# Layer 0 of a four-layer image kernel: sampled values through DRAM, two vertical taps in one matmul, and two small edits in layer 2

## The chip, the core and the metric

The kernel runs on one core of a Trainium2 chip. The metric is device time in microseconds (us), the median of several runs of the whole program. Five engines work side by side and meet only at semaphores: TensorE (PE, with its weight loads PEld), VectorE (DVE), ScalarE (ACT), GpSimd (POOL) and SyncE (SP, which here only issues DMA transfers). POOL issues DMA transfers as well.

## What is computed

Four residual layers run one after another on an image batch. Only layer 0 and layer 2 matter here. Layer 0 is a group norm, two 1x1 convolutions, and two deformable 3x3 convolutions of 180 channels in 10 groups of 18, on 2 images of 96x96:

```python
xr = conv1x1(x, w_reduce, b_reduce)
offs = conv1x1(xr, w_offset, b_offset)
off_w, off_h = (offs[:, :cm], offs[:, cm:])
f_w = deform_conv2d(xr, off_w, w_dcnw, b_dcnw)
f_h = deform_conv2d(xr, off_h, w_dcnh, b_dcnh)
...
val = gather(y0, x0, (1 - dy) * (1 - dx)) + gather(y0, x0 + 1, (1 - dy) * dx) + ...
patches = val.reshape(Bx, C, KK, Hx, Wx)
out = jnp.einsum('bikhw,oik->bohw', patches, weight.reshape(Cout, Cin, KK))
```

So each of the two convolutions (called cv = 0 and 1 in the kernel) samples every channel at 9 displaced places (taps) for each pixel, by bilinear weights, and then multiplies 180 channels x 9 taps by a weight matrix. Layer 2 is a bidirectional recurrence over 9216 positions (a running maximum and two running sums), a gate, a layer norm over channels and a 1x1 convolution.

## The kernel before

**Tiles of layer 0.** `near0` does one image. It walks 79 tiles of up to 128 positions: four of a narrow right edge (kind 2), 72 of 8 rows x 16 columns (kind 0; three make a chunk, two chunks a strip of 8 rows), three of the bottom edge (kind 1). Image 0 runs with the preparation of image 1 (`reduce0`, "aside") woven in; image 1 runs alone.

**Stages.** Each tile has three stages l = 0, 1, 2: groups 0-3, 4-7, 8-9. For a stage, POOL subtracts step positions from offsets (`hats`, L541), ACT turns that into hat weights (L548, L550), DVE multiplies vertical by horizontal weights (`products`, L571), PE transposes them into PSUM banks `pt` (`turn`, L587), ACT and DVE copy them out (L595, L593). `sample` then multiplies them on PE by 8x8 image windows `xw` (L634) for 8 patches of 4x4 pixels, and ACT copies the result from `pt` to `val` (L655): 8 copies of 288 columns in stages 0 and 1, 4 of 288 in stage 2, where two patches share a bank (`together`). There are five banks `pt`, which `turn` and `sample` share.

**Gathering.** A sampled group of 18 channels lies in its own 32 lanes. `gathered` moves it, SBUF to SBUF, on SP's queue (L672, L679): groups 0-6 into `main`, 126 lanes dense, groups 7-9 into `more`, three groups (54 lanes) at lane 0 for cv 0 and at lane 64 for cv 1. That is 26 transfers a tile, each of 18 lanes.

**Convolving.** `convolve` (L702) multiplies by the weights and accumulates in PSUM (`pf`), each tap at its own shifted place: 27 (output block, tap) pairs for `main` and 27 for `more`, both for cv 0 and cv 1 side by side, 128 columns each. It is a generator: in tile n+1, PE does the first half of tile n's `main` matmuls after stage 0's sampling, the second half after stage 1's, all of `more` after stage 2's. So per tile PE's order is: 36 transposes, sample 0, main, 36 transposes, sample 1, main, 18 transposes, sample 2, more.

**Orders.** In `near0` the order of PE, ACT and DVE is that of the program; POOL and SP are ordered by the scheduler. After each strip `done` and `finish` add borders, reduce, and let POOL add the bias and store the strip (L718 to L782). Windows for a later tile are 16 small DMA issues on POOL (`windows`, L559).

**Layer 2.** 18 chunks of 512 positions, each in three channel groups (54 iterations), forward and then backward. All four engines are in program order. `load` fetches the chunk's input `xt` (two buffers per image) six iterations ahead; in the backward half the gate reads the same `xt` (L1690 follows its matmul), so a buffer stays in use until its chunk's last gate. `weighted` (L1736) makes four exponentials on ACT (L1731, L1733): b, a, eb, ea. In the backward half a and ea share a ring of two PSUM banks, so the a of the next iteration waits until the scans of this one (L1755) have read theirs. Later on ACT in the same iteration come a logarithm and an exponential (`logged`, L1800, L1801), and DVE's `scaled` (L1813) waits for them.

Of the kernel before, what the change touches and what calls it, by code (L numbers as in the profile page):

```python
# [6 lines left out]
F32 = mybir.dt.float32  # L7
# [11 lines left out]
P = 128  # L19
CH = 96  # L20
CM, MH = 180, 90
# [13 lines left out]
LT = P  # L35
# [5 lines left out]
MAIN = 7  # L41
CO = 64
# [19 lines left out]
class Net:  # L62
# [283 lines left out]
    def near_constants(self, wn, at_d):  # L346
# [101 lines left out]
        wl = wn.tile([P, KK, NO * CO], F32, name="wl")  # L448
        nc.gpsimd.memset(wl, 0.0)
        nc.gpsimd.memset(wd[:, :, :, CM:], 0.0)  # L450
        for cv in range(2):
            src = ins["w_dcn"][cv].rearrange("(g t c) o -> g c t o", g=G, t=KK)
            for g in range(G):
                at = g * CG if g < MAIN else cv * 64 + (g - MAIN) * CG
                nc.gpsimd.dma_start(
                    out=wd[at : at + CG, cv, :, :CM] if g < MAIN else wl[at : at + CG, :, :CM],
                    in_=src[g],
                )
# [16 lines left out]
    def near0(self, b, xp_d, o_d, u_d, f_d, sums, far, top, con, aside=None):  # L475
# [5 lines left out]
        with ExitStack() as ctx:  # L481
# [4 lines left out]
            sv = ctx.enter_context(tc.tile_pool(name=f"n0v{b}", bufs=3))  # L486
# [111 lines left out]
            def split(kind, size, patches):  # L598

                rows, columns = size  # L600
                n = (len(patches) + 3) // 4
                return n, *((rows // n, columns) if kind != 1 else (rows, columns // n))

            def sample(sts, xw, l, kind, parts, patches):
# [8 lines left out]
                vals = []  # L613
                for e in range(2):
                    val = sv.tile([P, KK * LT], F32, name=f"val{e}")
                    vals.append(
                        val[:, : 2 * KK * rows * columns].rearrange(
                            "p (s r c) -> p s r c", r=rows, c=columns
                        )
                    )  # L620
                together = 1 if l < 2 else min(2, len(patches))
                for i in range(min(4, len(patches))):
# [24 lines left out]
                    for e in range(2):  # L647
                        to = vals[e][: nh * 64, :n]
                        if kind == 2:
                            to = to[:, :, vr : vr + together * nr]  # L650
                            to = to.rearrange("p s (j r) c -> p j s (r c)", j=together)
                        else:
                            to = to[:, :, :, vc : vc + together * ncol]
                            to = to.rearrange("p s r (j c) -> p j (s r) c", j=together)
                        nc.scalar.copy(  # L655
                            to,
                            pvs[e][: nh * 64, : together * w].rearrange(
                                "p (j a b) -> p j a b", j=together, b=to.shape[3]
                            ),
                        )  # L660
                return vals

            def gathered(main, more, l, vals, nh):

                for e in range(2):
                    val = vals[e].rearrange("p s r c -> p s (r c)")
                    for q in range(2):
                        g = 4 * l + (2 * q if l < 2 else 0) + e
                        for h in range(nh):
                            from_ = slice(h * 64 + q * 32, h * 64 + q * 32 + CG)  # L670
                            if g < MAIN:
                                nc.sync.dma_start(  # L672
                                    out=main[g * CG : (g + 1) * CG, h], in_=val[from_]
                                )
                                continue
                            for cv in range(2) if l < 2 else (q,):
                                lane = cv * 64 + (g - MAIN) * CG
                                s0 = cv * KK if l < 2 else 0
                                nc.sync.dma_start(  # L679
                                    out=more[lane : lane + CG, h], in_=val[from_, s0 : s0 + KK]  # L680
                                )

            def convolve(pf, main, more, kind, e, parts, first, last):

                nh, rows, columns = parts
                todo = [(m, t) for m in range(NO) for t in range(KK)]
                cut = len(todo) // 2
                for l, part in ((0, todo[:cut]), (0, todo[cut:]), (1, todo)):
                    for m, t in part:
                        ky, kx = 2 - t // 3, 2 - t % 3  # L690
                        y, x = ((ky, 16 * e + kx), (ky, 32 * e + kx), (32 * e + ky, kx))[kind]
                        for cv in range(2):
                            at = slice(cv * 64, cv * 64 + (G - MAIN) * CG) if l else slice(0, MAIN * CG)
                            wt = con["wl"][at, t] if l else con["wd"][:, cv, t]
                            if kind == 1:
                                to = pf[cv * CO : (cv + 1) * CO, m, y : y + rows, x : x + nh * columns]
                                to = to.rearrange("p r (h c) -> p h r c", h=nh)
                            else:
                                to = pf[cv * CO : (cv + 1) * CO, m, y : y + nh * rows, x : x + columns]
                                to = to.rearrange("p (h r) c -> p h r c", h=nh)  # L700
                            took = more[at, :, t] if l else main[:, :, cv * KK + t]
                            nc.tensor.matmul(  # L702
                                to,
                                wt[:, m * CO : (m + 1) * CO],
                                took.rearrange("p h (r c) -> p h r c", c=columns),
                                start=first and l == 0 and t == 0,
                                stop=last and l == 1 and t == KK - 1,
                                skip_group_check=True,
                                tile_position=(at.start, cv * CO),
                            )  # L710
                    yield

# [32 lines left out]
            ed = s1.tile([P, 3, H + 4, 4], F32, name="ed")  # L745
            nt = STRIPS * 6
            def plan(kind, i, j):
# [3 lines left out]
                for e in range(4 if kind == 2 else 3):  # L751
                    patches, corners = [], []
                    for a in range(8 if kind < 2 or e < 3 else 1):
                        r, c = a // (columns // 4) * 4, a % (columns // 4) * 4
                        y = (8 * i, W, 32 * e)[kind] + r
# [97 lines left out]
            for k, (n, l) in enumerate(stages):  # L853
# [15 lines left out]
                if k + 1 < len(stages):  # L869
# [4 lines left out]
                    make(turned + 1)  # L874
                if l == 0:
                    main = sb.tile([MAIN * CG, 2 * KK * LT], F32, name="main")
                    more = sb.tile([P, KK * LT], F32, name="more")
                    parts = split(kind, size, patches)
                    half = parts[1] * parts[2]
                    main, more = (  # L880
                        v[:, : parts[0] * m * half].rearrange("p (h s n) -> p h s n", s=m, n=half)
                        for v, m in ((main, 2 * KK), (more, KK))
                    )
                vals = sample(sts.pop(k), xws[n], l, kind, parts, patches)
                gathered(main, more, l, vals, parts[0])
# [609 lines left out]
    def layer2(self, x, out, stats):  # L1495
# [10 lines left out]
        with ExitStack() as ctx:  # L1506
# [5 lines left out]
            sy = ctx.enter_context(tc.tile_pool(name="l2y", bufs=2))  # L1512
            pk = ctx.enter_context(tc.tile_pool(name="l2k", bufs=2, space=PSUM))
# [141 lines left out]
            def load(i):  # L1655
                back, c, g = seq[i]
                if g == 0:
                    xts[back, c] = []
                    for b in range(B):
                        xt = sb.tile([CH, 2, T], F32, name=f"xt{b}")  # L1660
# [75 lines left out]
            def weighted(i):  # L1736
                if seq[i][0]:
# [756 lines left out]
```

## Time and profile before

The kernel takes 10528.72 us (median of 3 runs, 10526.48 to 10530.25). The profiled execution took 10534.88 us, with a span of 10533.1 us from first to last instruction. Busy time by stretch of the span:

| stretch (us) | what | length | PE | DVE | ACT | POOL | PE clock | DMA share | GB/s |
|---|---|---|---|---|---|---|---|---|---|
| 0-390 | layer 0, preparation | 390 | 190 | 188 | 14 | 59 | 0.84 | 0.74 | 133 |
| 390-3030 | layer 0, image 0 | 2640 | 2515 | 2057 | 1673 | 1781 | 0.98 | 0.38 | 91 |
| 3030-5205 | layer 0, image 1 | 2175 | 2135 | 1599 | 1502 | 1369 | 0.99 | 0.37 | 90 |
| 5205-6115 | end of layer 0, layer 1 | 910 | 617 | 567 | 116 | 179 | 0.81 | 0.39 | 117 |
| 6115-6465 | layer 2, forward | 350 | 243 | 315 | 311 | 266 | 0.92 | 0.49 | 168 |
| 6465-7150 | layer 2, backward | 685 | 536 | 570 | 441 | 513 | 0.85 | 0.39 | 117 |
| 7150-10533 | layer 3 | 3383 | 3130 | 2963 | 1952 | 2845 | 0.85 | 0.71 | 163 |

How to read the profile: "PE L702 MATMUL pf<-more,wl 54*64 54x128" is the instruction at line 702, its output and inputs by the program's names, the weight's shape and the moving operand's (lanes x columns). A float32 matmul shows as two instructions, a transpose as one. Brackets at the end of a timeline line give how long the engine stood still before it and what ended that. The share of DMA is the mean over 16 DMA engines; "issue" lines on SP and POOL show how long an engine took to issue transfers, not how long these took.

### The profile page before, as it was taken

To read this page: it belongs to the slowest core of one execution; us is meant where nothing else is said; L and a number is where in the kernel's file an instruction comes from. 1 tells how busy PE (TensorE), PEld (TensorE's weight loads), DVE (VectorE), ACT (ScalarE), POOL (GpSimd) and SP (SyncE) were. 2 spreads that over 40 slices of the span, in tenths; PEclk is the share of its full clock that TensorE was granted. 3 is DMA by queue.
4 is the path that set the end of the run, shared out by engine and by line. 5 is a ranking of instruction groups with operands and counts; after the bars stand their busy time and mean duration, and the time that the engine had idled before them with its cause. 6 is when DMAs were issued, how large, how long until landed. Compare 5 with 4: busy or idle time off the path is not lost. (4 is left out here: it accounts for less than half of the span.)

```text
span 10533.1 us, 230262 instructions
## 1 busy us (share of the span) xinstructions
PE 9365.6 (89%) x92614; PEld 5530.4 (53%) x92614; DVE 8257.2 (78%) x8704; ACT 6008.3 (57%) x11216; POOL 7013.2 (67%) x5527
## 2 busy tenths in 40 slices
PE   4799999999989999999966776787999999999998
PEld 3588888888868888888822222222222222222222
DVE  4677777777677777777755788883999999999999
ACT  0366666666666676666600168663666666666664
POOL 1466766766555666666511258773888888888888
PEclk8899999999989999999978888886888888888887
DMA  8433434433323333333344344432777777777776
GB/s 146 90 93 95 97 96 95 97 96 95 78 68 89 93 90 91 89 93 90 80 128 127 109 153 150 123 120 72 170 172 170 172 171 172 173 170 171 172 169 148
DMA packets 601281, 1282.72 MB, mean 122 GB/s; under 512 B 238700, under 2 KB 321888, under 8 KB 543808
## 3 DMA queue, kind: packets, MB, share of 16 engines
q1 hardware_dynamic: 387560, 1081.12, 41.7%
q0 software_dynamic: 103808, 133.18, 5.7%
q10 hardware_dynamic: 108840, 53.57, 2.0%
q8 instruction: 739, 12.11, 0.5%
q14 instruction: 334, 2.74, 0.1%
HBM read 786.57 MB, written 231.25 MB: 97 GB/s over the span
## 5 line engine op out<-in xcount | busy, mean ns | idle before, releaser
L571 DVE TENSOR_TENSOR sp<-h 128x2304 f32<-128x2304 f32 x790 | 2162.2, 2769 | 25.7 <-ACT h L550 25.7
L2236 DVE TENSOR_TENSOR_SCAN h<-da,state,bu 128x512 f32<-128x512 f32 x1632 | 1959.5, 1262 | 238.2 <-ACT da L2226 231.9
L595 ACT COPY st<-pt 128x512 f32<-128x512 f32 (+1 forms) x2370 | 1218.7, 517 | 1310.3 <-PE pt L587 1241.3
L2203 POOL TENSOR_TENSOR bu<-bu,bs 128x2048 f32<-128x2048 f32 x432 | 1954.0, 4523 | 16.9 <-DMA bu<-ud 16.8
L593 DVE COPY st<-pt 128x512 f32<-128x512 f32 x1580 | 1062.0, 687 | 985.2 <-PE pt L587 968.3
L587 PE MATMUL pt<-ident,sp 128*128 128x128 f32 x14220 | 1679.4, 276 | 97.9 <-DVE sp L571 56.6
L541 POOL TENSOR_TENSOR h<-u,step 128x1152 f32<-128x1152 f32 (+1 forms) x474 | 1202.5, 2551 | 816.6 <-DVE u L514 464.0
L587 PEld LDWEIGHTS pt<-ident,sp 128*128 128x128 f32 x14220 | 1565.8, 142 | 185.7 <-issue 93.0
L559 POOL DMA_DIRECT2D xw<-xp_d x2500 | 1393.4, 632 | 142.2 <-PE pt L634 83.1
L2226 ACT ACTIVATE da<-da,nA 128x512 f32<-128x512 f32 x1728 | 1048.9, 662 | 657.8 <-PE da L2212 656.5
L634 PE MATMUL pt<-st,xw 64*32 64x288 f32 (+1 forms) x30000 | 1075.8, 367 | 77.0 <-ACT st L595 30.9
L655 ACT COPY val<-pt 128x288 f32<-128x288 f32 (+1 forms) x3132 | 986.1, 398 | 209.3 <-PE pt L634 205.5
L2212 PE MATMUL da<-dl,spread 32*128 32x512 f32 x3456 | 984.7, 692 | 15.3 <-DVE h L2236 7.5
L702 PE MATMUL pf<-more,wl 54*64 54x128 f32 (+1 forms) x17064 | 958.2, 268 | 10.9 <-DMA more<-val 10.2
L702 PEld LDWEIGHTS pf<-main,wd 126*64 126x64 f32 x17064 | 889.6, 137 | 140.7 <-issue 132.5
L702 PE MATMUL pf<-main,wd 126*64 126x128 f32 (+1 forms) x17064 | 962.1, 270 | 1.0 <-DMA main<-val 0.3
L702 PEld LDWEIGHTS pf<-more,wl 54*64 54x64 f32 x17064 | 920.4, 136 | 48.1 <-issue 34.7
L634 PEld LDWEIGHTS pt<-st,xw 64*32 64x32 f32 x30000 | 541.1, 106 | 483.2 <-ACT val L655 172.8
L2259 DVE TENSOR_TENSOR hc<-h,cc 128x1536 f32<-128x1536 f32 x432 | 747.1, 1729 | 0.0
L2104 PE MATMUL pe<-xn,sb_w_in 96*128 96x512 f32 x864 | 572.2, 797 | 113.1 <-ACT xi L2112 63.4
L2270 POOL TENSOR_TENSOR hp<-h,cs 128x512 f32<-128x512 f32 x432 | 550.2, 1274 | 163.7 <-PE da L2212 96.5
L2212 PEld LDWEIGHTS da<-dl,spread 32*128 32x128 f32 x3456 | 300.6, 193 | 667.1 <-DVE h L2236 433.6
(338 smaller groups left out, 12827.6 us busy)
## 6 DMA issues: line engine op xcount, KB each, us to landing
bu<-ud SPq DMA_DIRECT2D x432, 1024.0 KB
main<-val SPq DMA_DIRECT2D x2016, 81.0 KB
more<-val SPq DMA_DIRECT2D x1728, 40.5 KB
xw<-xp_d POOLq DMA_DIRECT2D x2500, 26.0 KB
xt<-x_d SPq DMA_DIRECT2D x108, 384.0 KB
half_d<-hv SPq DMA_DIRECT2D x54, 768.0 KB
hv<-half_d SPq DMA_DIRECT2D x54, 768.0 KB
u_d<-u SPq DMA_DIRECT2D x158, 180.0 KB
```

What stands on the lines that cost most here:

```text
L541: nc.gpsimd.tensor_tensor(hs, u[:, :, 8 * KK * l : 8 * KK * l + n].unsqueeze(3).to_broadcast([P, 2, n, WS]), con["step"].unsqueeze(1).unsq ...
L559: nc.gpsimd.dma_start(out=xw[e * WN : (e + 1) * WN, i], in_=xp_d[y : y + WS, x : x + WS, e * CM // 2 : e * CM // 2 + XW],)
L571: nc.vector.tensor_tensor(sp.rearrange("p s (y x) -> p s y x", x=WS), hy.unsqueeze(3).to_broadcast([P, n, WS, WS]), hx.unsqueeze(2).to_bro ...
L587: nc.tensor.transpose(pt[:, q], sp[:, 2 * (q0 + q) : 2 * (q0 + q) + 2].rearrange("p e w -> p (e w)"), self.ident,)
L593: nc.vector.tensor_copy(st[:, q0 : q0 + m], pt[:, :m])
L595: nc.scalar.copy(st[:, q0 : q0 + m], pt[:, :m])
L634: nc.tensor.matmul(pvs[e][lane : lane + 32, j * w : (j + 1) * w], xw[e * WN : (e + 1) * WN, win, g * CG : g * CG + 32], sts[pair][e * WN : ...
L702: nc.tensor.matmul(to, wt[:, m * CO : (m + 1) * CO], took.rearrange("p h (r c) -> p h r c", c=columns), start=first and l == 0 and t == 0, ...
L2203: nc.gpsimd.tensor_tensor(bu, bu, got[s]["bs"].unsqueeze(1).to_broadcast([P, 4, T]), ALU.mult)
L2212: nc.tensor.matmul(das[r], spread[at, v].rearrange("p n e -> p (n e)"), got[s]["dl"][at, i], start=True, stop=True, tile_position=(32 * r, 0),
L2226: nc.scalar.activation(da, da, AF.Exp, scale=nA[:, 4 * q + r : 4 * q + r + 1])
L2236: nc.vector.tensor_tensor_scan(h[:, r], got[s]["da", q][r], bu[:, r], init, ALU.mult, ALU.add)
```

## The change

In layer 0 three things change together, and in layer 2 two.

- **The way of the samples.** `val` becomes six fixed buffers, one pair per stage, in which each tap's block has one row of pixels more than before, a row of zeros ahead (cleared by POOL whenever the tile's shape changes). `gathered` writes whole halves of `val` (64 lanes, gaps included) to DRAM on SP: 4 writes each in stages 0 and 1, 2 of 128 lanes in stage 2. `main` is then read back as 126 dense lanes in two transfers, issued by POOL; `more` in 12 transfers of 18 lanes, issued by SP. Two sets of DRAM buffers alternate.
- **Two taps in one matmul.** `more` now holds the three last groups twice in its 118 lanes: at lane 0 and at lane 64 with different taps, whose vertical places differ by one row. A tap below another is the same output place one row of pixels further on, so with the zero row one matmul over 9 rows (2 x 9 x 8 = 144 columns) does two of the three vertical taps; the third is a matmul of 128 columns. For cv 0 and cv 1 side by side that makes 18 pairs for `more` in place of 27 (27 in kind 2, where each half of the tile is done alone). Main's 27 pairs stay.
- **Places by columns.** A tile of kind 0 is halved by columns (8 x 8 and 8 x 8) in place of rows (4 x 16 and 4 x 16). In stage 2 of kinds 0 and 1 patches no longer share a bank: 8 copies of 144 columns in place of 4 of 288.
- **Layer 2.** The input tiles `xt` get three buffers in place of two, and in the backward half `weighted` makes eb ahead of a.

```diff
-                return n, *((rows // n, columns) if kind != 1 else (rows, columns // n))
+                return n, *((rows // n, columns) if kind == 2 else (rows, columns // n))
...
-                together = 1 if l < 2 else min(2, len(patches))
+                together = 1 if l < 2 or kind < 2 else min(2, len(patches))
...
-                                nc.sync.dma_start(
-                                    out=main[g * CG : (g + 1) * CG, h], in_=val[from_]
-                                )
...
+                if l < 2:
+                    to = stored(far_m, nh, 8, 32, 2 * size)
+                    for e in range(2):
+                        q = 4 * l + 2 * e
+                        for h in range(nh):
+                            nc.sync.dma_start(
+                                out=to[h, q : q + 2].rearrange("q c n -> (q c) n"),
+                                in_=vals[e][h * 64 : (h + 1) * 64, : 2 * size],
+                            )
+                    if l == 0:
+                        return
+                    for h in range(nh):
+                        nc.gpsimd.dma_start(out=main[:, h], in_=to[h, :MAIN, :CG])
...
+                            nc.sync.dma_start(
+                                out=more[lane : lane + CG, :, slot * third : slot * third + w],
+                                in_=bass.AP(
+                                    to.tensor,
+                                    starts[cv].offset + s0,
+                                    [[wide, CG], [apart, nh], [1, w]],
+                                ),
+                            )
...
-                for l, part in ((0, todo[:cut]), (0, todo[cut:]), (1, todo)):
...
+                for alone in range(2):
+                    for m in range(NO):
+                        for t in range(3):
+                            for h in range(nh) if kind == 2 and not alone else (None,):
+                                for cv in range(2):
+                                    at = 64 * cv * alone
+                                    lanes = slice(at, at + REST if alone else 64 + REST)
+                                    slot = 1 if alone else 2 * cv
+                                    took = more[lanes, :, (3 * slot + t) * one :][:, :, :one]
...
+                                        blocks(took, cv * alone, rows + 1 - alone),
...
+            for more in mores:
+                nc.gpsimd.memset(more, 0.0)
...
+                if shapes[l] != (kind, parts):
+                    shapes[l] = (kind, parts)
+                    for val in roles[l]:
+                        nc.gpsimd.memset(val, 0.0)
...
-                        xt = sb.tile([CH, 2, T], F32, name=f"xt{b}")
+                        xt = sx.tile([CH, 2, T], F32, name=f"xt{b}")
...
             def weighted(i):
+                weight(i, "b", sb, "b2", -1.0, w)
                 if seq[i][0]:
-                    weight(i, "b", sb, "b2", -1.0, w)
+                    weight(i, "eb", sb, "eb", -1.0, nu)
                     weight(i, "a", pa, "e", 1.0, ew)
                 else:
-                    weight(i, "b", sb, "b2", -1.0, w)
                     weight(i, "a", pm, "pm", 1.0, ew)
-                weight(i, "eb", sb, "eb", -1.0, nu)
+                    weight(i, "eb", sb, "eb", -1.0, nu)
                 weight(i, "ea", pa, "e", 1.0, u)
```

## The prediction

> **What bounds the kernel now.** The page first. PE is busy 89% of the span, and at 9 tenths or more in nearly every slice of layer 0 (the first half):
>
> ```profile
> PE 9365.6 (89%) x92614; PEld 5530.4 (53%) x92614; DVE 8257.2 (78%) x8704; ACT 6008.3 (57%) x11216; POOL 7013.2 (67%) x5527
> PE   4799999999989999999966776787999999999998
> ...
> L702 PE MATMUL pf<-more,wl 54*64 54x128 f32 (+1 forms) x17064 | 958.2, 268 | 10.9 <-DMA more<-val 10.2
> ```
>
> The last line is the work that the change shortens: 958 us of PE, with only 10.9 us of waiting. Next the timeline of PE over one tile of image 1:
>
> ```profile
> 4009.84 1.26 PE L634 MATMUL pt<-st,xw 64*32 64x144 f32 x64
> 4011.03 6.16 PE L702 MATMUL pf<-more,wl 54*64 54x128 f32 x108
> 4017.12 4.15 PE L587 MATMUL pt<-ident,sp 128*128 128x128 f32 x36
> 4021.20 2.65 PE L634 MATMUL pt<-st,xw 64*32 64x288 f32 x64
> 4023.78 3.06 PE L702 MATMUL pf<-main,wd 126*64 126x128 f32 x52
> ```
>
> No brackets: PE never stands still, and a tile takes 28.8 us from one `more` block to the next (31.0 in image 0). So what PE gains or loses counts in full, until something else is late. What POOL does meanwhile, in a plain tile and at a strip's end:
>
> ```profile
> 4011.49 8.87 POOL L559 DMA_DIRECT2D xw<-xp_d  x16 [1.20 <-PE pt L634]
> 4024.63 5.49 POOL L541 TENSOR_TENSOR h<-u,step 128x1152 f32<-128x1152 f32 x2 [4.28 <-ACT val L655]
> ...
> 4150.40 2.17 POOL L541 TENSOR_TENSOR h<-u,step 128x1152 f32<-128x1152 f32 x1
> 4153.68 1.87 POOL L781 COPY fa<-fa 128x600 f32<-128x600 f32 x1
> 4158.94 2.10 POOL L782 MEMSET fa<- 128x2400 f32 x1
> ```
>
> In a plain tile POOL waits often; at a strip's end its step product at L541 comes without slack. In layer 2 the waits of the backward half and the chain there:
>
> ```profile
> ACT e L1733 <- DVE opq L1755: 197.4, 51, 6.8
> DVE nd L1813 <- ACT r L1801: 75.4, 51, 7.8
> PE k L1605 <- DMA xt<-x_d: 46.7, 13, 7.0
> ```
>
> ```profile
> 6797.88 5.56 DMA xt<-x_d
> 6803.57 3.75 PE k L1605 x4
> 6807.32 3.23 PE pm L1834 x8
> 6810.58 0.70 ACT rs L1843
> 6813.06 0.70 DVE nd L1813
> ```
>
> DVE is the busiest engine there, and what holds it is ACT's late result, itself behind a late load of `xt`.
>
> **1. More's matmuls: -259 us.** 108 instructions are 54 matmuls in 27 pairs: 6.16/27 = 0.228 us a pair; main's are 3.06/13 = 0.235. The 64-column pairs of image 0's bottom edge take 1.74/13 = 0.134, so a column costs (0.235 - 0.134)/64 = 0.0016 us. Afterwards 9 pairs of 144 columns at 0.235 + 16 x 0.0016 = 0.260 and 9 of 128 at 0.228: 4.39 us, 1.77 less. Times 144 tiles of kind 0: -255; the six of kind 1 give some -4; kind 2 keeps 27 pairs. Short runs of pixels cost nothing visible: those 0.134 us pairs write runs of 2.
>
> **2. Sample 2: +105 us.** Eight copies need eight banks where four did, with five banks in all; PE must wait for ACT. The nearest row is the bottom edge's stage 0, of the same shape with eight copies:
>
> ```profile
> 2964.49 2.04 PE L634 MATMUL pt<-st,xw 64*32 64x144 f32 x64
> 2965.14 1.91 ACT L655 COPY val<-pt 128x144 f32<-128x144 f32 x8 [0.17 <-PE pt L634]
> ```
>
> 2.04 against 1.26: at most 0.78, at least 0 if the banks come free in time. I take 0.7, near the row, for 150 tiles: +105. ACT's own 0.6 us more (1.91 against 1.30) is hidden by the `more` block, in which ACT stands still 4.42 us.
>
> **3. POOL's two reads of main: +41 us at strips' ends.** Two issues of 0.55 us (16 xw in 8.87) to 0.77 (an o_d issue in image 0), some 1.4 us, hidden in a plain tile by the 12 us in which POOL waits. The order of instructions shows them in image 0 after the last L541 and ahead of the windows; in image 1 after the first window issue. Behind them stand windows, then L541, for which ACT and then DVE and PE wait. In image 1 the order also puts, at a strip's end, two stores (1.14), the copy (1.87), the clearing (2.10) and three window issues (1.7) ahead of the L541 that comes at 4150.40: up to 6.8 us later. ACT takes that result at 4153.20, right after it is made. Part of it lies beside a wait of 1.81 us that PE has there anyhow, and DVE's products are late already: between 0 and 6.8 for 12 strips; I take 2 (24 us). Image 0: 1.4 x 12 = 17 us, between 0 and 30.
>
> **4. SP's queue: 0.** 22 transfers in place of 26. The reads of `more` wait for writes of the same stage, ahead of the next tile's writes; u_d and raw go before them. At the 0.72 us of an issue, 22 take 16 us of 27.8, and two round trips of some 3 us fit. `more` is wanted a tile later. Without that cover the next writes, and main, would be late: see the rivals.
>
> **5. Start, change of shape, end: +45 us.** POOL clears two `more` and six `val` at the start of each image: 128x2400 took 2.10 us, so 128x1296 takes 1.13: 8 us on image 1's start, where PE waits for windows (27.73 us in the trace); image 0's lie beside the preparation. Three changes of shape an image clear pairs of buffers before ACT may copy (2.3 us a pair), and the last tile waits for two trips through DRAM with nothing beside them, some 10 us. Between 15 and 90; I take 45.
>
> **6. Layer 2: -60 us.** The third buffer lets `xt` come a chunk (38 us) earlier, and eb (0.71 + 0.63) is done in ACT's wait instead of after it. Both shorten what L1813 waits for. Its 75.4 us are the upper end; the lower is 20, if the second of two things that end together stays. DVE's work in a chunk is some 33.8 us of 38.0 (three iterations of 10.2 to 11.8 without waits), so about 60 of 75.
>
> The weight loads (12 more small transfers on POOL) fall into the preparation, where POOL works 59 of 390 us: 0.
>
> **Sum.** -259 + 105 + 41 + 45 - 60 = -128 on the profiled 10,534.9: 10,407; the median lies 6 us under that execution: **10,401 us**.
>
> **Is main in time?** This decides. With t = 0 at a tile's first main matmul (3994.93), stage 1's copies end at 10.4 and SP has issued its writes by 13.3; in the packet records a first packet follows an issue by 1.4 us, so they land near 16. POOL's reads follow sample 2, at 17.6 to 19.0; data from 19; wanted at 27.8. They bring 1.31 MB, beside 0.66 MB of stage 2's writes and 0.42 MB of windows. How fast? Two stretches bound it:
>
> ```profile
> 5336.00:5342.00 6.00, 0.00 (x0) 0.00 (x0) 5.93 (x2) 0.00 (x0) 0.00 (x0) 0.50 1.01 423
> 4005.00:4034.00 29.00, 29.00 (x506) 25.17 (x504) 20.61 (x21) 20.70 (x44) 16.53 (x19) 1.00 0.37 88
> ```
>
> The last two columns are DMA share and GB/s: 423 at a full share for large loads, 88/0.37 = 238 for today's traffic. 2.39 MB take 5.6 us or 10.0: done at 24.6 or 29.0, against 27.8. Image 0 issues later (20.5 to 21.9 of 30): 27.5 or 31.9. The new rows of 5,184 bytes are large and one side of each is DRAM, like the loads of the first stretch, so I forecast in time.
>
> The Trainium skill speaks against this: DMA: Bandwidth & Descriptors, "Why a DMA increments its semaphore by 16 and not by 1", says that a transfer gets as many engines as the largest number up to 16 that divides the slowest dimension of both sides. The read of main goes over 7 groups into 126 lanes, so 7 engines. By a sixteenth of 423 GB/s each, 0.65 MB would take an estimated 3.5 us, or 7.1 for both on the same seven, done at 26.1 with nothing beside. No row here shows which engines work; the sum would stay as it is.
>
> **Rivals.** (a) *Main comes late*, the one on the slower side: at 238 GB/s 1.2 us too late in image 1, 1.9 in image 0, 72 tiles each: +223, so 10,624. For it: DMA share would go from 0.37 to some 0.7 to 0.9 (5.2 MB a tile for main and more in place of 1.6). Against it: the first stretch above. From 0.9 us a tile the gain is gone. (b) *The gain is whole*: sample 2 costs 0.3 and strips nothing: -259 + 45 + 30 - 70 = -254, so 10,275. For it: ACT stands still after sample 2; against it: the bottom edge's row. (c) *It cancels*: strips at 5 us in both images (+120 for 41) and sample 2 at 0.78: -37, so 10,492, and with layer 2 at its lower end 10,532: no change. For it: POOL's missing slack at strips' ends.
>
> **How the numbers follow.** Forecast (10,340 to 10,480) 0.50, (a) 0.23, (b) 0.13, (c) 0.14. A measurement tells 0.2% (21 us) from no change: below 10,508 is faster. The forecast, (b) and a third of (c) lie there, 0.67; 0.09 within; (a) and a little of (c) above, 0.24. The range goes from 10,290, near (b), to 10,650, over (a); the forecast's own is 10,340 to 10,480.
>
> **What would show it.** Right: a `more` block of 4.4 us, sample 2 near 2.0, a plain tile of 27.8 (image 0: 30.0), no PE wait for main, no wait of PE for `xt`, L1813's wait under 20 us. Wrong: PE waiting for DMA main in every tile; POOL waiting for far_m ahead of its windows; a `more` block above 5; strips' ends that cost more than 8 us over a plain tile.

## The result and the profile after

The changed kernel is slower: 11,095.15 us (median of 4 runs, 11,090.59 to 11,132.88) against 10,528.58 us (median of 4, 10,526.48 to 10,530.25) for the kernel before, a ratio of 1.0549 with a 95% interval of 1.0528 to 1.057. The forecast was 10,401 us, and the range ended at 10,650. The profiled execution of the changed kernel took 11,132.9 us, of the kernel before 10,534.9; by stages of their traces (an image of layer 0 from the first transpose of `turn` to the last):

| stage | before | after | difference |
|---|---|---|---|
| image 0 of layer 0 | 2495.9 | 2824.6 | +328.7 |
| from image 0 to image 1 | 58.4 | 61.0 | +2.6 |
| image 1 of layer 0 | 2321.6 | 2619.3 | +297.7 |
| end of layer 0, layer 1 | 876.3 | 890.7 | +14.4 |
| layer 2, forward | 331.0 | 327.9 | -3.1 |
| layer 2, backward | 662.7 | 625.3 | -37.4 |
| layer 3 | 3412.8 | 3409.7 | -3.1 |

So layer 0 lost some 640 us and layer 2 gained 40. The page of the changed kernel, its busy times, the busy tenths of PE and of the DMA engines in 40 slices, and four of its groups:

```profile
PE 9404.3 (84%) x87142; PEld 5443.6 (49%) x87142; DVE 8364.0 (75%) x8704; ACT 6056.3 (54%) x11816; POOL 6936.6 (62%) x5905
...
PE   4689888888878888888885677788799999999998
...
DMA  8466666667646676766664434443477777777776
...
L569 POOL DMA_DIRECT2D xw<-xp_d x2500 | 1391.0, 589 | 1250.6 <-DMA main<-far_m 1029.4
...
L643 PE MATMUL pt<-st,xw 64*32 64x288 f32 (+1 forms) x30000 | 1193.4, 378 | 315.1 <-ACT st L605 211.1
L765 PE MATMUL pf<-main,wd 126*64 126x128 f32 (+1 forms) x17064 | 1100.9, 293 | 357.5 <-DMA main<-far_m 326.0
...
L786 PE MATMUL pf<-more,wl 118*64 118x144 f32 (+5 forms) x11592 | 737.1, 279 | 0.2
```

The first three of these groups in the kernel before:

```profile
L559 POOL DMA_DIRECT2D xw<-xp_d x2500 | 1393.4, 632 | 142.2 <-PE pt L634 83.1
...
L634 PE MATMUL pt<-st,xw 64*32 64x288 f32 (+1 forms) x30000 | 1075.8, 367 | 77.0 <-ACT st L595 30.9
...
L702 PE MATMUL pf<-main,wd 126*64 126x128 f32 (+1 forms) x17064 | 962.1, 270 | 1.0 <-DMA main<-val 0.3
```

In layer 0 PE fell from 9 tenths to 8, and the DMA digits stand at 6 and 7. The number behind the last arrow is the idle time that the named cause ended: PE waited 326 us for main, and POOL, which issues the windows, 1029 us for the same thing. For PE the two pages add up: the main matmuls gained some 357 us of standing and 139 of longer blocks, sampling 238 of standing and 118 of work, and the `more` block gave back some 220. Together that is nearly the whole loss of layer 0. The two reads themselves cost POOL what was forecast (1.29 us for both, below). PE over one tile of image 1 of the changed kernel:

```profile
4336.10 2.03 PE L643 MATMUL pt<-st,xw 64*32 64x144 f32 x64
4338.06 4.72 PE L786 MATMUL pf<-more,wl 118*64 118x144 f32 x72
4342.70 4.15 PE L597 MATMUL pt<-ident,sp 128*128 128x128 f32 x36
4346.78 2.65 PE L643 MATMUL pt<-st,xw 64*32 64x288 f32 x64
4353.22 5.81 PE L765 MATMUL pf<-main,wd 126*64 126x128 f32 x52 [3.79 <-DMA main<-far_m]
```

The block of `more` is shorter, 4.72 us for 6.16, and sample 2 longer, 2.03 for 1.26. But PE stands still 3.79 us before main, and the block of main takes 5.81 us in place of 3.06: PE starts when the first half is there and waits again inside for the second. POOL in the same tile:

```profile
4338.51 0.57 POOL L569 DMA_DIRECT2D xw<-xp_d  x1 [1.74 <-DMA u_d<-u]
4339.20 1.29 POOL L704 DMA_DIRECT2D main<-far_m  x2
4340.48 1.69 POOL L569 DMA_DIRECT2D xw<-xp_d  x3
4344.06 1.66 POOL L569 DMA_DIRECT2D xw<-xp_d  x3 [1.88 <-issue]
4350.91 0.55 POOL L569 DMA_DIRECT2D xw<-xp_d  x1 [5.19 <-DMA main<-far_m]
4353.45 4.41 POOL L569 DMA_DIRECT2D xw<-xp_d  x8 [2.00 <-DMA main<-far_m]
```

The reads go out right after sample 2, as forecast. Six windows follow. The seventh stands 5.19 us until main's first half has landed, and the eighth until the second has. In the list of instructions POOL's transfers take turns on eight completion semaphores (104 to 111): the first read has 111, and the window that stands at 4350.91 takes 111 again. So the eighth transfer after a read waits for that read, and a slow read stops POOL, which issued it. In a plain tile POOL has time for that; at a strip's end it has not:

```profile
4438.75 0.69 POOL L892 COPY fa<-fa 128x600 f32<-128x600 f32 x1
4439.38 0.61 POOL L569 DMA_DIRECT2D xw<-xp_d  x1
4439.98 2.12 POOL L893 MEMSET fa<- 128x2400 f32 x1
4442.02 0.59 POOL L569 DMA_DIRECT2D xw<-xp_d  x1
4442.61 5.47 POOL L551 TENSOR_TENSOR h<-u,step 128x1152 f32<-128x1152 f32 x3
...
4433.92 2.18 PE L597 MATMUL pt<-ident,sp 128*128 128x128 f32 x18
4447.83 2.63 PE L643 MATMUL pt<-st,xw 64*32 64x144 f32 x64 [11.72 <-ACT st L605]
```

The windows that waited for main stand between the pieces of the strip's end, L551 comes last, and PE stands still 11.72 us for what follows from it. At one strip's end of the kernel before, PE's longest stop at sample 2 was 1.81 us:

```profile
4160.04 1.35 PE L634 MATMUL pt<-st,xw 64*32 64x144 f32 x62 [1.81 <-DVE st L593]
```

From one `more` block to the next a plain tile of image 1 takes 29 to 37 us (mostly 28.8 before), a strip's end 42 to 46 (33.7 to 34.5 before). The plain tiles are many, so they carry more of the loss: in image 1 they make 176 us and the strips' ends 109, in image 0 245 and 38.

### The profile page after: what moved, and what is told of

It is laid out like the page before. It is cut to its first block, busy times and chain, and to the rows that moved or that the text cites. A ratio compares the mean times of both kernels' runs of the same rounds, so it can differ in the third digit from the quotient of the medians.

```text
span 11130.6 us, 219256 instructions
## 1 busy us (share of the span) xinstructions
PE 9404.3 (84%) x87142; PEld 5443.6 (49%) x87142; DVE 8364.0 (75%) x8704; ACT 6056.3 (54%) x11816; POOL 6936.6 (62%) x5905
## 5 line engine op out<-in xcount | busy, mean ns | idle before, releaser
L581 DVE TENSOR_TENSOR sp<-h 128x2304 f32<-128x2304 f32 x790 | 2202.9, 2820 | 202.3 <-ACT h L560 202.3
L569 POOL DMA_DIRECT2D xw<-xp_d x2500 | 1391.0, 589 | 1250.6 <-DMA main<-far_m 1029.4
L603 DVE COPY st<-pt 128x512 f32<-128x512 f32 x1580 | 1066.5, 689 | 1331.0 <-PE pt L597 1317.4
L643 PE MATMUL pt<-st,xw 64*32 64x288 f32 (+1 forms) x30000 | 1193.4, 378 | 315.1 <-ACT st L605 211.1
L765 PE MATMUL pf<-main,wd 126*64 126x128 f32 (+1 forms) x17064 | 1100.9, 293 | 357.5 <-DMA main<-far_m 326.0
L765 PEld LDWEIGHTS pf<-main,wd 126*64 126x64 f32 x17064 | 1028.1, 152 | 506.5 <-issue 359.1
L551 POOL TENSOR_TENSOR h<-u,step 128x1152 f32<-128x1152 f32 (+1 forms) x474 | 899.0, 1932 | 460.8 <-DVE u L524 431.0
L668 ACT COPY val<-pt 128x288 f32<-128x288 f32 (+1 forms) x3600 | 1014.1, 363 | 277.2 <-PE pt L643 263.4
L2328 PE MATMUL da<-dl,spread 32*128 32x512 f32 x3456 | 957.1, 696 | 15.4 <-DVE h L2352 7.2
L786 PE MATMUL pf<-more,wl 118*64 118x144 f32 (+5 forms) x11592 | 737.1, 279 | 0.2
L786 PEld LDWEIGHTS pf<-more,wl 118*64 118x64 f32 (+1 forms) x11592 | 669.4, 138 | 70.6 <-issue 51.3
L558 ACT ACTIVATE h<-h 128x1152 f32<-128x1152 f32 (+1 forms) x474 | 482.2, 1017 | 306.6 <-POOL h L551 306.6
```

The lines of the kernel that those rows point to most:

```text
L569: nc.gpsimd.dma_start(out=xw[e * WN : (e + 1) * WN, i], in_=xp_d[y : y + WS, x : x + WS, e * CM // 2 : e * CM // 2 + XW],)
L581: nc.vector.tensor_tensor(sp.rearrange("p s (y x) -> p s y x", x=WS), hy.unsqueeze(3).to_broadcast([P, n, WS, WS]), hx.unsqueeze(2).to_bro ...
L603: nc.vector.tensor_copy(st[:, q0 : q0 + m], pt[:, :m])
L643: nc.tensor.matmul(pvs[e][lane : lane + 32, j * w : (j + 1) * w], xw[e * WN : (e + 1) * WN, win, g * CG : g * CG + 32], sts[pair][e * WN : ...
L765: nc.tensor.matmul(place(cv, m, 2 - t // 3, 2 - t % 3, None, 0), con["wd"][:, cv, t, m * CO : (m + 1) * CO], blocks(took, 1, rows), start= ...
L786: nc.tensor.matmul(place(cv, m, 2 * cv if alone else 1 - cv, 2 - t, h, 1 - alone,), con["wl"][lanes, slot, t, m * CO : (m + 1) * CO], bloc ...
```

## The experiments

Theory 1 is that main's read through DRAM comes late and does all the harm, at PE (1a, the transfer) and through POOL (1b, what stands behind it). Against it stand the traffic through DRAM as a whole, POOL's new order, sample 2's copies and SP's queue. Each comparison has its own runs of the kernel before (medians 10,514.4, 10,516.9, 10,515.5 and 10,520.9 us), so ratios are given.

**Without the read of main, and with main gathered as before.** The first run leaves out main's two reads:

```diff
-                    for h in range(nh):
-                        nc.gpsimd.dma_start(out=main[:, h], in_=to[h, :MAIN, :CG])
```

> The changed kernel without the two reads of main from DRAM: main is cleared once and stays zero, so groups 0 to 6 add nothing to the convolutions. Theory 1 (main's read is late, at PE directly and at POOL, whose windows stand behind it): both waits vanish, the plain tile of image 1 goes from about 32 us to 28 and a strip's end from 45 to about 36; 10,430 to 10,480 us. Theory 2 (the writes and reads through DRAM as a whole hold up everything, or sample 2's eight copies and the new order on POOL do): without this one read the time stays above 10,800.

10,409.0 us, ratio 0.9893 (0.9878 to 0.9908): all of the loss is gone. A plain tile of image 1 mostly takes 28.2 us and a strip's end 32.0. The second run keeps main whole, copied from SBUF to SBUF, while `more` still goes through DRAM:

```diff
+                                if g < MAIN:
+                                    nc.sync.dma_start(out=main[g * CG : (g + 1) * CG, h], in_=from_[:CG])
+                                else:
+                                    nc.sync.dma_start(out=to[h, g], in_=from_)
```

> The changed kernel with main gathered from SBUF to SBUF on SP, 18 lanes at a time, as before; only group 7 and stage 2, which make more, go through DRAM. Theory 1 (main's late read): 10,430 to 10,500 us, no wait of PE or POOL for main. Theory 2 (DRAM traffic as a whole): the trips of more remain, so a part of the loss remains, above 10,600. A third possibility, SP's queue (18 issues more a tile than the changed kernel has for main): more comes late, PE waits for it, 10,500 to 10,700.

10,466.7 us, ratio 0.9952 (0.9937 to 0.9967): theory 1 holds. Gathering main directly costs 58 us against no main at all, and the traffic of `more` through DRAM, which both runs have, leaves both under the kernel before. (The 18 further issues of the expectation were miscounted: 16 transfers stand where 8 writes stood.)

**The same read, issued by SP.**

```diff
-                        nc.gpsimd.dma_start(out=main[:, h], in_=to[h, :MAIN, :CG])
+                        nc.sync.dma_start(out=main[:, h], in_=to[h, :MAIN, :CG])
```

> The changed kernel with main's two reads issued by SP, behind the writes they wait for, in place of POOL. Theory 1a (the transfer of some 9 us is too slow by itself): PE still waits for main, 326 us in the changed kernel, less what an issue 1 to 3 us earlier brings; POOL's 1029 us of waiting at the windows go; 10,600 to 10,850 us. Theory 1b (POOL's blocked windows make the loss): 10,430 to 10,550. Theory 2 (DRAM traffic as a whole): nothing changes, 11,000 to 11,150.

10,635.4 us, ratio 1.0119 (1.0103 to 1.0134), in the range of 1a: some 450 us of the loss go away when SP issues the read. SP, then PE, in this run:

```profile
4309.09 1.77 SPq L704 DMA_DIRECT2D main<-far_m  x2
...
4317.41 2.65 PE L643 MATMUL pt<-st,xw 64*32 64x288 f32 x64
4320.35 3.06 PE L765 MATMUL pf<-main,wd 126*64 126x128 f32 x52 [0.29 <-DMA main<-far_m]
```

The read is as slow as before. But it goes out sooner in the tile (in image 1 the middle half of the issues stands 16.5 to 18.0 us after the tile's first main matmul, on POOL 18.7 to 21.0), and no window stands behind it. So here it is 0.29 us late in place of 3.79 above. This run does not tell these two apart.

**What makes the read 9 us long.** Four runs change its shape. In two parts, issued by POOL and then by SP:

```diff
+                    for h in range(nh):
+                        last = min(4 * l + 4, MAIN)
+                        nc.gpsimd.dma_start(
+                            out=main[4 * l * CG : last * CG, h], in_=to[h, 4 * l : last, :CG]
+                        )
                     if l == 0:
                         return
```

> The changed kernel with main read in two parts, still by POOL: groups 0 to 3 (72 lanes) as soon as stage 0's writes are there, groups 4 to 6 (54 lanes) after stage 1's. Theory 1a (the 9 us of the transfer): the part that is left at the critical place is 0.56 MB of 1.31, about 4 us, so it lands near 24 of the tile's 28 us, PE no longer waits and POOL's windows wait 0 to 2 us a tile; 10,470 to 10,600. Theory 1b (POOL as the issuing engine, whatever the size: two more issues a tile, and windows behind a read that waits): above 10,750.

10,961.7 us, ratio 1.0425 (1.0407 to 1.0442), in the range that the expectation gave to 1b and far above what the bytes promise. The second part holds 0.56 MB, less than half, and PE still stood still for it:

```profile
4333.38 0.61 POOL L703 DMA_DIRECT2D main<-far_m  x1 [1.96 <-DMA far_m<-val]
4334.24 0.60 POOL L703 DMA_DIRECT2D main<-far_m  x1 [0.25 <-issue]
...
4343.63 3.06 PE L768 MATMUL pf<-main,wd 126*64 126x128 f32 x52 [1.89 <-DMA main<-far_m]
```

> Main read in two parts as above, but issued by SP, so that POOL waits for neither. From the run with the whole read on SP (10,635.4 us, of which some 120 stand in image 0): the second part of 0.56 MB lands 4 to 5 us earlier, so the 33 us of PE's waiting in image 1 go. Theory A (image 0's loss of 120 us is also main's lateness): 10,450 to 10,500. Theory B (image 0's loss comes from DRAM traffic beside the preparation of image 1, or from DVE there): 10,570 to 10,620.

11,263.7 us, ratio 1.0711 (1.0693 to 1.0729), outside what either theory gave: in SP's one queue the read of the first part also stands ahead of writes of stage 1. In one tile SP issued the last of those at 4327.42 and the second read only at 4334.43. How those 7 us divide was not followed further.

Half the bytes over the same seven groups, on POOL:

```diff
-                        nc.gpsimd.dma_start(out=main[:, h], in_=to[h, :MAIN, :CG])
+                        nc.gpsimd.dma_start(out=main[:, h, :size], in_=to[h, :MAIN, :CG, :size])
```

> The changed kernel, in which POOL's two reads of main fetch only the values of cv 0: half the bytes, over the same 7 groups and as many packets (2,592 bytes in place of 5,184); cv 1's half of main stays zero, so groups 0 to 6 are missing from the second convolution. Theory 1a (the bytes and the busy DMA engines make the read last 9 us): it lands some 4 us sooner, PE's wait for main goes, POOL's 1029 us at the windows fall under 400; 10,480 to 10,650 us. Theory 1c (the number of DMA engines that a read gets by its groups, and the fixed time until a read starts, make it long, whatever the bytes, as the run in two parts with 10,961.7 us hints): less than half of the loss goes; above 10,750.

10,591.0 us, ratio 1.0076 (1.0059 to 1.0093), as theory 1a has it: PE waits 24 us for main in place of 326, and POOL 319.5 in place of 1029.4. That POOL's wait does harm by itself shows here too: nearly all strips' ends of image 1 still take 37 to 39 us, against 32.0 for most without the read. One thing in the expectation is not so: the records have 126 packets of 5,184 bytes a tile in place of 252, and not as many packets of half the size. So this run halves bytes and packets together.

Dense rows in DRAM and one read of 126 rows, issued by SP:

```diff
-                    to = stored(far_m, nh, 8, 32, 2 * size)
+                    to = stored(far_m, nh, MAIN * CG + 32, 2 * size)
...
+                                    out=to[h, g * CG : g * CG + m],
+                                    in_=vals[e][h * 64 + q * 32 : h * 64 + q * 32 + m, : 2 * size],
...
+                    nc.sync.dma_start(out=main, in_=to[:, : MAIN * CG].rearrange("h c n -> c h n"))
```

> The kernel with main's read issued by SP (10,635.4 us), but the samples of stages 0 and 1 are written in 18 lanes a group, without the 14 lanes between groups, dense in DRAM, and main is read in one transfer of 126 rows of two pieces. Bytes of these writes fall from 2.65 to 1.6 MB a tile; 8 more issues on SP. Theory 1c (a read gets engines by the slowest dimension, 126 rows in place of 7 groups): up to 14 packets of one transfer are in flight at a time, and the read takes 6 us or less from first to last packet in place of 8 to 9. Time: 10,550 to 10,650 if SP's queue bears the 8 issues; above 10,700 if it does not.

10,490.0 us, ratio 0.9978 (0.9968 to 0.9988), better than both expected cases, and 0.2% faster than the kernel before: through DRAM, main can be in time. Counted from the packet records of one tile each, the packets of main's read that were under way together, and the time from the first packet to the last:

```
run                issued by   slowest dimension    under way together       first to last packet
changed kernel     POOL        7 groups, 2 reads    10 to 15 after 1.5 us    9.5 us (median of 45 tiles)
main_sp            SP          7 groups, 2 reads    7                        9.0 us
main_split, 2nd    POOL        3 groups, 2 reads    3, then 5 to 6           8.0 us, for 43% of the bytes
dense_sp           SP          126 rows, 1 read     13 to 15                 5.0 us (all but a last few)
```

So on SP's queue the length goes with the packets under way, 7 or 14, and their number follows the groups, not the lanes (dense_sp also writes fewer bytes and reads in one transfer, not two). The Trainium skill has this in DMA: Bandwidth & Descriptors, "Why a DMA increments its semaphore by 16 and not by 1": a transfer gets as many engines as the largest number up to 16 that divides the slowest dimension of both sides, always the lowest-numbered engines for SP's transfers, and in turn round the sixteen for POOL's. By it the two reads on SP share 7 engines, those on POOL get 14 between them, a read of 3 groups gets 3 and one of 126 rows 14. These records agree, if a packet under way stands for an engine; they name no engine.

On POOL the 10 to 15 were no faster than the 7 on SP: a packet of 5,184 bytes took 353 ns on average there and 200 to 245 ns through most of the read on SP. POOL's queue alone does not make that difference. In the run main_dense below POOL issues the dense read, with next to no other packet beside it, and there the median packet took 199 ns and the read some 5.5 us. So in the changed kernel it is what runs at the same time, the two reads on POOL and on average four other packets. Why these slow it while some five others beside the read on SP do not is not shown.

**POOL's place for the read.** First the changed kernel with POOL in the order of the program:

```diff
                         mybir.EngineType.DVE,
+                        mybir.EngineType.Pool,
```

> The changed kernel with POOL in the order of the program: main's reads stand ahead of the step product of stage 2 (L551), and the windows come after it. The transfer is the same. Theory 1a (transfer): PE's wait for main stays near 300 us in all; 10,800 to 11,050. Theory 1b (what stands behind main on POOL makes most of the loss): with some 3 us of other work between main and the windows, POOL's wait of 1029 us falls by a third or more and the strips' ends come down from 45 to about 38 us; 10,600 to 10,800.

11,995.2 us, ratio 1.1401 (1.1382 to 1.142), far outside both: of the 1500 us from 3500 on, POOL stands 448.5 us at these reads until stage 1's writes have landed. Second, the dense read on POOL (`nc.gpsimd` for `nc.sync` in the last line of the diff of dense_sp):

> The dense writes and the single read of main of 126 rows (10,490.0 us when SP issues it), with the read issued by POOL. The order of instructions puts it on POOL ahead of the third step product (L551) of a tile, 16 windows later than that. If only the length of the read (5 us in place of 9) matters: 10,480 to 10,560. If POOL pays for standing at the read until stage 1's writes have landed, with the step product behind it: above 10,700, with POOL's wait for far_m as its largest.

12,779.2 us, ratio 1.2149 (1.213 to 1.2167), on the side of POOL's place. POOL of the run in program order, then SP, POOL and PE of the run with the dense read:

```profile
4327.98 0.64 POOL L704 DMA_DIRECT2D main<-far_m  x1 [13.70 <-DMA far_m<-val]
```

```profile
4301.26 3.52 SPq L699 DMA_DIRECT2D far_m<-val  x8
...
4321.76 5.49 POOL L551 TENSOR_TENSOR h<-u,step 128x1152 f32<-128x1152 f32 x2 [3.74 <-DVE sp L581]
4327.20 0.80 POOL L705 DMA_DIRECT2D main<-far_m  x1
...
4335.22 4.41 PE L766 MATMUL pf<-main,wd 126*64 126x128 f32 x52 [15.21 <-DMA main<-far_m]
```

In the first, POOL stands 13.70 us at the read until its data are written, with the next step product and 16 windows behind it. In the second it is the other way round, and not as I had expected: the data went out at 4301 to 4305, but 16 windows and two step products stand ahead of the read on POOL, which issues it at 4327, and PE waits 15.21 us. The length of the read, some 5.5 us, is not what makes this run slow. One and the same read makes 10,490 us issued by SP and 2,289 us more issued by POOL.

**What was left in image 0.** With the read on SP, image 1 takes 2,325.7 us (2,321.6 before), but image 0 still 2,614.3 (2,495.9 before). DVE there from 600 to 2,800 us, in the run with main gathered directly and in the run with the read on SP:

```profile
L116 DVE TENSOR_SCALAR xn<-xt,gn_s,gn_b 96x128 f32<-96x128 f32 x128 | 85.9, 736 | 0.0
```

```profile
L116 DVE TENSOR_SCALAR xn<-xt,gn_s,gn_b 96x128 f32<-96x128 f32 x128 | 174.3, 1446 | 0.0
```

The same 128 instructions of image 1's preparation take twice as long; the median of one is 335 ns. PE's wait for DVE's copies (L603) in image 0 is 96.6 us there, against 26.1 with main gathered directly. The next run makes them on ACT:

```diff
+                if queue is nc.gpsimd:
+                    nc.scalar.activation(
+                        xn[:, k],
+                        xt[:, k],
+                        AF.Identity,
+                        bias=gn[1][:, k : k + 1],
+                        scale=gn[0][:, k : k + 1],
+                    )
```

> The kernel with main's read issued by SP (10,635.4 us), in which the preparation of image 1 beside image 0 makes its normalized input xn on ACT in place of DVE. In that run xn (335 ns on DVE alone) took 3.0 us on average where POOL's step product ran beside it, 174 us of DVE from 600 to 2800 us in place of 86 with main gathered directly. Theory A (this is image 0's loss of some 120 us): image 0's 2614 us become 2490 to 2520, the whole 10,510 to 10,550. Theory B (image 0 loses to DRAM traffic in another way): 10,600 to 10,640.

10,460.9 us, ratio 0.9953 (0.9939 to 0.9967), 174 us less than with xn on DVE; image 0 takes 2,443.9. Theory A holds, with more than the size it gave. Image 0 gains 170 us. With main gathered directly and patches in pairs the same edit gains 53 there (below), so some 117 would be left for the meeting with POOL, and 118 was the loss to explain.

**Sample 2 undone, and the gains together.** Two patches share a bank again, laid so that one copy serves both:

```diff
-                together = 1 if l < 2 or kind < 2 else min(2, len(patches))
+                together = 1 if l < 2 or kind == 1 else min(2, len(patches))
...
+                                if together == 2 and kind == 0:
+                                    to = pvs[e][lane : lane + 32, : 2 * w].rearrange(
+                                        "p (s r c) -> p s r c", s=n, r=nr
+                                    )[:, :, :, j * ncol : (j + 1) * ncol]
```

> The kernel with main gathered from SBUF to SBUF (10,466.7 us) and, beside it, stage 2's patches of kind 0 in pairs again: two patches share a bank, so that four copies of 288 columns do what eight of 144 did. Theory A (PE bounds the plain tile, and sample 2 stands there for five banks): sample 2 goes from 2.03 to about 1.27 us, 0.77 less for 144 tiles, 10,340 to 10,380 us. Theory B (DVE's or ACT's copies bound the tile once main is in time): the time only moves to another wait, 10,440 to 10,470.

10,374.1 us, ratio 0.9864 (0.9848 to 0.9881), theory A. PE's sample 2 in this run:

```profile
4327.43 1.26 PE L648 MATMUL pt<-st,xw 64*32 64x144 f32 x64
```

> The kernel with main gathered directly and stage 2 in pairs (10,374.1 us), with xn of image 1's preparation on ACT in place of DVE. DVE loses some 86 us of work in image 0, 50 of it spent waiting beside POOL's step product. If DVE's copies hold PE in image 0: 10,320 to 10,355; if not, 10,365 to 10,380.

10,322.4 us, ratio 0.9819 (0.9802 to 0.9835): DVE does hold PE in image 0, which falls from 2,448.7 to 2,395.5.

> The dense writes and the single read by SP (10,490.0 us), with stage 2 in pairs (worth 92.6 us with main gathered directly) and xn on ACT (worth 51.8 there, 174.5 with the gapped read on SP). If the gains add: 10,260 to 10,345. If SP's queue or the DMA engines bound it once PE is faster: 10,360 to 10,450.

10,319.4 us, ratio 0.9815 (0.98 to 0.983): the gains add, and the two ways of main now come to the same. Both versions beat the kernel before and the changed one.

**Layer 2 alone, and each of its edits alone.**

> The kernel before with the two edits in layer 2 alone (three buffers for xt, eb ahead of a). From the stages of the changed kernel's trace (layer 2 forward 331.0 to 327.9, backward 662.7 to 625.3) I expect 10,488 us, 10,475 to 10,500. If the gain in the changed kernel was only a shift of work that came late from layer 0, the time stays within 10,520 to 10,535.

10,481.2 us, ratio 0.9966 (0.9954 to 0.9978), 33 us less.

> The kernel before with three buffers for xt alone. The wait of PE for xt was 46.7 us of the trace of before (13 times), ahead of ACT's late result. If xt carries layer 2's gain of 33 us: 10,482 to 10,492; if the order does: 10,508 to 10,518.

10,507.6 us, ratio 0.9989 (0.998 to 0.9998).

> The kernel before with eb ahead of a alone. If the order carries the gain: 10,482 to 10,492; if xt does: 10,508 to 10,518. If both are needed (ACT's result is late for either reason), neither run gains more than 12 us.

10,503.5 us, ratio 0.9979 (0.997 to 0.9988). Each gives a part (13 and 17 us; by the intervals 2 to 21 and 13 to 32), and neither carries the gain alone. The waits of DVE in the backward half, before and with both edits (from 6465 to 7120 us and over the same stage):

```profile
DVE nd L1813 <- ACT r L1801: 69.1, 47, 7.8
DVE yo L1883 <- PE pm L1873: 20.0, 12, 2.8
```

```profile
DVE yo L1884 <- PE pm L1874: 39.9, 22, 3.4
...
DVE nd L1814 <- ACT r L1802: 3.4, 6, 1.0
```

The wait for ACT is gone, but 20 us of it came back as a longer wait for PE's last product.

## Why the prediction was wrong

**The step that failed** is the paragraph "Is main in time?", with its conclusion "so I forecast in time". It weighed 423 GB/s against 238 and took the first, because the rows are long and one side is DRAM. At 423 GB/s read and other traffic take 5.6 us. With the read on POOL 9.5 us went by from first packet to last, at 193 GB/s for all traffic and a DMA share of 0.86 (4340 to 4351 us of the trace), so neither long rows nor DRAM on one side gave the rate of the first stretch. The first packet came some 2.1 us after the issue, not 1.4. In image 1 the two halves were there some 11 and 12 us after their issues, and in most tiles PE waited 1.3 to 4 us. That is the end that I had named and not taken.

The sentences on 7 engines would not have turned it. They priced both reads at 7.1 us with nothing beside, done at 26.1 and so in time. They also put both reads on the same seven, which the quoted rule says of SP's transfers and not of POOL's; in the records 10 to 15 packets were under way.

**The rival "main comes late" had the right place and too small a price.** It gave 10,624, counting only how late main is for PE: 1.2 and 1.9 us a tile. PE's bare wait was 326 us, some 2.3 a tile, and the blocks of main grew by another 139 where its second half came later still. What no term or rival of the prediction held is the other half: POOL's windows behind the read, 1029 us of POOL's waiting, and with it L551 and PE at the strips' ends (211 us of PE's standing in 25 places). Only its signs of being wrong named dear strips' ends. Moving the read to SP, which also sends it out sooner, takes away some 450 us, though the read stays as slow.

**Term 3, POOL's reads at strips' ends (+41 us),** counted their issues, and 1.29 us for both is what they took. The waiting for their landing was missing: a strip's end of image 1 costs 10 to 14 us over a plain tile of some 32, against 5 before.

**Term 1 (-259)** has the right mechanism, 18 pairs, and too large a size. The block took 4.6 to 4.7 us, not 4.39, so 1.4 to 1.5 us less a tile in place of 1.77, or 206 to 222 us over 144 tiles where I had 255.

**Term 2 (+105)** held: sample 2 at 2.03 us, 0.77 more (I took 0.7), and undoing it brought back 92.6 us, 0.64 for each of 144 tiles.

**Term 4 (0)** held: PE waited 0.2 us at the `more` block in the changed kernel.

**Term 5 (+45)** was too high, near its lower bound of 15: the passage between the images grew by 2.6 us and the end of layer 0 with layer 1 by 14.4. What the clearings cost inside the images was not split off.

**Term 6 (-60)** is half in size: 33 us by itself (40.5 between the two traces). The lower bound had been argued as "the second of two things that end together"; what took the place was a third, DVE's wait for PE's product at the end of the chunk.

**The sum** itself stood without the read: the run that leaves it out took 10,409.0 us, a ratio of 0.9893, against 0.9879 forecast. That agreement is in part luck. This run also lacks the two issues of term 3 (+41), so the terms left add up to -169, and it gained 105 to 113: terms 1 and 6 promised some 60 to 80 us too much between them, and term 5 charged some 28 too much. What stands is that layer 0 and layer 2 gain when main costs nothing, and that the one question that the prediction called decisive was answered wrongly.

## What to carry to other kernels

Price a DMA that something waits for from its issue to its landing under the traffic of its own stage, and look at the slowest dimension of its access pattern: issued by SP, 126 lanes cut as 7 groups of 18 had 7 packets under way, and the same lanes as 126 dense rows had 14. Before giving a slow read to an engine that also computes, list what stands ahead of it and behind it on that engine: the place of one and the same read made a difference of 2,289 us. When an engine that runs beside another becomes later or earlier, look at which instructions of the two now meet.

## What the hardware showed that I had not expected

**More packets at a time did not make the read faster on POOL.** Two reads with 7 packets under way (SP) took 9.0 us, and with 10 to 15 (POOL) 9.5, with stage 2's writes ahead of them and the windows beside them. The share of the DMA engines in image 1 was 0.67 at 179 GB/s, in the kernel before 0.37 at 90.

**A DVE instruction took nine times as long beside POOL's.** With the read on SP the normalization xn (335 ns in the median) took 3.0 us on average, and up to 5.6, in the 53 cases in which POOL's step product L551 filled most of its time. The Trainium skill, SBUF — State Buffer, "Who interferes with whom", says that such a DVE instruction in its two-port form and a GpSimd instruction share a pair of ports: whichever is issued first has it for its whole length, and the other stands still. The trace fits that: 51 of the 53 ended 0.08 or 0.09 us after a step product. It also goes beyond it: 49 of the 53 met two step products and one met three that followed one another on POOL, and nearly all ended only after the last, so DVE did not get in between them. That longest one, 5.59 us from 410.01, lasted through products from 410.00 to 415.51. In the kernel before, 57 of 75 met one product alone, and xn took 0.95 us on average in the 75; how far into L551 the two met was not measured.
